# Attention over gathered tokens on one core: one transpose for the reciprocal sums of two pairs of heads, and the norms of the first of two pairs moved later

## The chip, the cores and the metric

The kernel runs on one core of a Trainium2 chip. The metric is the device time of one execution in microseconds; lower is better. An engine is named as the profile names it: PE is TensorE, DVE is VectorE, ACT is ScalarE, POOL is GpSimd, and SP is the engine whose queue issues most of the transfers. PEld is the weight load of TensorE, which overlaps its products.

## The reference, cut to what matters

There are B = 16 sequences (called batches here) of T = 1024 tokens with D = 512 features. A mask of zeros and ones marks about half of the tokens of each. The same projection serves as query, key and value, for 8 heads of 64 features:

```python
q = xt @ Wq.T                                     # (B, T, D)
qh = q.reshape(B, T, NH, dk).transpose(0, 2, 1, 3)
scores = scale * jnp.einsum('bhqd,bhkd->bhqk', qh, qh)
logits = (scores * cmask + (1.0 - cmask) * NEG) * rmask
attn = jax.nn.softmax(logits, axis=-1)
ctx = jnp.einsum('bhqk,bhkd->bhqd', attn, qh)
out = ctx @ Wo.T                                  # (B, T, D), added to x
```

A masked key gets no weight. A masked query has all logits zero, so its row is the plain mean over all tokens. Only the unmasked tokens need the attention proper.

## The kernel before, in words

**Tiles.** For each batch the unmasked tokens (at most C = 544) are gathered to the front: four full tiles of 128 rows and a tail of 32. Heads are worked on in pairs: 8 heads are 4 pairs, numbered p = 0 to 3, and a group g of four heads is two pairs (0 and 1, or 2 and 3). The scores of one head and one tile of 128 rows are a block of 128 x 544, made on PE by products in fp16 of a high and a low part (`scores`, L611), then exponentiated on ACT with a sum along the row (L615). The tails of four heads are packed into one such block (L586, L590) and split by DVE into two parts (L595, L596), which four transfers `pt` spread (L602, L603). `attend` multiplies the probabilities by the values: L629 for the full tiles, L632 for the tails. ACT then copies the context of the pair, still without the division by the row sums, to a tile `c` of 128 x 544 (L636): its partitions are the 2 x 64 features of the pair, its columns the tokens.

**The division.** The sums lie along the partitions (one token to a partition), but the context needs them along the columns. Three steps do this for each pair:

- `recip_sums` (L644) puts the corrected sums of the pair into ten columns of a tile `rcol` (128 x 128) and takes the reciprocals, on DVE: two heads, five blocks of tokens each.
- `recip_rows` (L661) transposes the whole `rcol` by a product with the identity (L665), copies the ten rows that matter to `rr` (L668), writes them to DRAM (`rd`, L670) and reads them back with two transfers (`rb`, L673), each of which broadcasts one head's 544 values over 64 partitions. `rb` has two buffers.
- `norm` (L677) multiplies `c` by `rb` (L696), puts the means of padded queries in (L697), and splits the result into a high and a low half in fp16: `ch` and `cl` for the full tiles (L699, L700), a column block of `ct` for the tail (L701, L702). For pairs 0 to 2 the multiplication also waits for the last score or query product issued before it (`self.beat`).

`project` multiplies `ch` and `cl` by the output weights (L712, 12 products a tile of 128 rows, three for each pair), DVE adds the old x (L717), and POOL scatters the rows. `project_tail` does the same for the tails of a group of up to three batches.

**The order of the work.** `run` goes through the batches in one software pipeline. A batch has 18 slots, four for each pair and two for the packed tails (slots 2 and 13). In each slot the scores of two heads are issued; between them come the products of the block before (`attend`), and a share of the list `m`. That list holds the rest: query blocks (L443) and their transposes to values (L489) of the next batch, the gathered x of the next batch transposed (L420) and split (L380 on ACT, L381 on DVE), and the projection of the batch before. Steps in `free` are tied to a slot and come before its scores. For pairs 0 and 1 and 2 the sums come two slots after the pair's last, the rows three, and the norm of pairs 0 and 1 seven. The norm of pair 2 (`second`) and sums, rows and norm of pair 3 (`sums`, `rows`, `third`) are done in the next batch:

```python
m = sums + pk(b, 1) + x[:2] + second + x[2:4] + rows + x[4:]
```

and later `third` stands between two parts of query block 1: `q(1, 0) + v(0) + third + q(1, 1)`. A query block ends with a mask that DVE applies to columns 384 to 543 (L449); the transpose of the fourth column block waits for it. The last batch has its own list, and `last` ends the kernel.

The calls give a rough order only. A scheduler then places the instructions on each engine, moving ready ones ahead of waiting ones; what is marked with `high_priority` (the copy `rr`, the splits of x, the addition L717) goes first. Once placed, each engine works in that fixed order and waits at the head of its queue. All transfers named above are in the one queue of SP.

Of the kernel before, what the change touches and what calls it, by code (L numbers as in the profile page):

```python
# [10 lines left out]
F32 = mybir.dt.float32  # L11
# [8 lines left out]
P = 128  # L20
# [3 lines left out]
DK = 64  # L24
NP = H // 2
DC = D // P
# [4 lines left out]
C = 544  # L31
# [18 lines left out]
class Fast:  # L50
# [593 lines left out]
    def recip_sums(self, b, p):  # L644

        nc, s = self.nc, self.st[b]
        hs, g = slice(2 * p, 2 * p + 2), p // 2
        corr = s["corr"][g]
        r = self.rcol[p % 2][:, :10]
        m = r.rearrange("p (h k) -> p h k", k=5)  # L650
        nc.vector.tensor_tensor(m[:, :, :4], s["z"][:, hs, :],
                                corr[:, p % 2 * 2:p % 2 * 2 + 2].unsqueeze(2).broadcast_to([P, 2, 4]), ALU.subtract)
        for h in range(2):
            q = (2 * p + h) % HG
            rows = slice(q * CT, (q + 1) * CT)
            nc.vector.tensor_tensor(m[:CT, h, 4:5], s["zt"][rows, g:g + 1], corr[rows, HG:], ALU.subtract)
        nc.vector.tensor_scalar(r, r, 1e-35, 1.0 / SX, ALU.max, ALU.mult)
        nc.vector.reciprocal(r, r)
        nc.vector.tensor_tensor(m, m, self.hit[:, b, :].unsqueeze(1).broadcast_to([P, 2, 5]), ALU.mult)

    def recip_rows(self, b, p):  # L661

        nc, s = self.nc, self.st[b]
        pt = self.pm([P, P])
        nc.tensor.transpose(pt, self.rcol[p % 2], self.ident)  # L665
        rr = self.sb([10, P], F32, "rr", 2)
        with self.tc.high_priority(offset=HPO):
            nc.vector.tensor_copy(rr, pt[:10])  # L668
        rd = self.dram.tile([10, P], F32, tag="rd", name="rd")
        nc.sync.dma_start(out=rd, in_=rr)  # L670
        rb = self.sb([P, C], F32, "rb", 2)
        for k in range(2):
            nc.sync.dma_start(out=rb[k * DK:(k + 1) * DK, :], in_=rd[5 * k:5 * k + 5, :].rearrange("k t -> (k t)")[:C]  # L673
                              .unsqueeze(0).broadcast_to([DK, C]))
        s.setdefault("rb", {})[p] = rb

    def norm(self, b, p):  # L677
        nc, s = self.nc, self.st[b]
# [127 lines left out]
    def last(self, b, todo):  # L806

        for f in self.soon + todo:
            f()
        self.soon = []  # L810
        while self.urgent or self.spare:
            self.issue()
        self.paced = False
        s = self.st[b]
        self.recip_sums(b, 3)
        pos = []
        for i in range(2):
            t = self.ps_s.tile([P, 2, D], F32, tag="s", name="pss")
            pos += [t[:, k, :] for k in range(2)]
        pos.append(self.pm([P, D]))  # L820
        for i in range(4):
            self.product(s["ch"], s["cl"], slice(i * P, (i + 1) * P), pos[i], range(3))
            if i == 0:
                self.recip_rows(b, 3)
        self.norm(b, 3)
        for i in range(4):
            self.project(b, i, pos[i], range(3, DC))
        self.project_tail(b, pos[4])

    def run(self, flag):  # L830
        B = self.B
        L = lambda f, *a: lambda: f(*a)
# [3 lines left out]
        N = len(S)  # L836
# [93 lines left out]
        if True:  # L930
            for b in range(B + 1):
                o, n = b - 1, b + 1
# [2 lines left out]
                    break  # L935
                free, sums, rows, third, tail, rest = {}, [], [], [], [], []
                if b:
                    sums, rows, third = [(0, L(self.recip_sums, o, 3))], [(0.1, L(self.recip_rows, o, 3))], [(0, L(self.norm, o, 3))]
                if n < B:
                    if b in tails:  # L940
                        free[0] = [L(self.late, o, 4)]
# [1 line left out]
                    for x in rests.get(b, []):  # L943
                        free.setdefault(0, []).extend(L(self.late, x, j) for j in range(5, 9))
                        rest += [(0, L(self.rest, x, j)) for j in range(5, 9)]
                second = [(0, L(self.norm, o, 2))] if b else []
                P_ = (lambda *i: project(o, *i)) if b else (lambda *i: [])
                pk, tp, bt = ((lambda o, g, f=f, c=c: [(c, L(f, o, g))]) for f, c in ((self.peaks, 0), (self.top, 0.1), (self.bottom, 0.1)))
                new = [g for g in groups if b == g[0] - 2], [g for g in groups if b == g[0] - 1]
                if n < B:  # L950
                    q, x, v = (lambda e, g: query(n, e, g)), xt(n)[2 if b == 0 else 0:], (lambda e: value(n, e))
                    tc, tv = ((lambda g, f=f, c=c: [(c, L(f, n, g))]) for f, c in ((self.tail_copy, 0), (self.value_tail, 0.25)))
                    rng = [(0, L(self.range_x, n, c)) for c in range(DC)]
                    ahead = b + 2 < B
                    hot, index = ([(c, L(f, b + 2))] if ahead else [] for f, c in ((self.hot, 0), (self.index, 0.2)))
                    take = [(0, L(self.gather, b + 2, j)) for j in range(5)] if ahead else []
                    m = sums + pk(b, 1) + x[:2] + second + x[2:4] + rows + x[4:]
                    for g in new[0]:
                        m += [(0, L(self.active, *g))]
                    m += q(0, 0) + tp(b, 1) + q(0, 1)  # L960
                    for g in new[0]:
                        m += [(0.3, L(self.slots, *g))]
                    for g in new[1]:
                        m += [(0, L(self.facts_sums, *g))]
                    m += bt(b, 1) + q(1, 0) + v(0) + third + q(1, 1)
                    for g in new[1]:
                        m += [(0.1, L(self.facts_end, *g))]
                    m += tc(0) + rng[:2] + tail + v(1) + P_(0) + tv(0) + rest + P_(1) + hot + rng[2:] + q(2, 0) + index
                    m += pk(n, 0) + q(2, 1) + tp(n, 0) + P_(2) + take + v(2) + q(3, 0) + bt(n, 0)
                    m += q(3, 1) + tc(1) + [(0, L(self.means, n))] + P_(3) + v(3) + tv(1)  # L970
                    if b == 0:
                        k = next(k for k, (c, f) in enumerate(m) if f is index[0][1])
                        for c in range(DC):
                            m.insert(k + 1 + 3 * c, (0, L(self.split, "o", c)))
                else:

                    places = [("xi", 8), ("xa", 13)]
                    come = [[L(self.late, x, j, *places[k % 2]) for j in range(5, 9)] for k, x in enumerate(rests[b])]
                    leave = [[L(self.rest, x, j) for j in range(5, 9)] for x in rests[b]]
                    free[0] = [L(self.late, b, 4)] + come[0]  # L980
                    for c, l in zip(come[1:] + [[]], leave):
                        free[0] += c + l
                    m = second + sums + pk(b, 1) + [(2.6, L(self.project_means, b))] + rows + [(0.6, lambda: None)]
                    m += tp(b, 1) + [(0.6, lambda: None)] + bt(b, 1) + [(1.2, lambda: None)] + third + [(1.2, lambda: None)] + P_(0, 1, 2, 3)
                if b == 1:
                    m += [(0, L(self.range_w, "o", c)) for c in range(DC)]
# [2 lines left out]
                if b == 0:  # L989
                    m = begin + m  # L990
# [22 lines left out]
                for st, (p, i) in enumerate(S):  # L1013
                    soon, self.soon = self.soon, []
                    for f in soon + free.get(st, []):
                        f()
                    if i is None:
                        self.scores(b, p, None)
                    else:
                        ps = [self.scores(b, 2 * p, i)]  # L1020
                        if i == 2 and whole:
                            whole.pop()()
                    fill(share[st][0], st == N - 1)
                    if i is not None:
                        ps.append(self.scores(b, 2 * p + 1, i))

                    for _ in range(1 if b < B - 2 else -(-len(self.urgent + self.spare) // (N - st))):
                        self.issue()

                    if i in (0, 2):  # L1030
                        ready, todo = todo, []
                    elif i in (1, 3):
                        for f in ready[1::-1] + ready[2:]:
                            f()
                        ready = []
                    fill(share[st][1])
                    if i is not None:
                        todo.append(L(self.attend, b, p, i, ps))
                    if i == 3:
                        (whole if p < 3 else todo).append(L(self.attend, b, p, 4, None))  # L1040
                        if p < 3:
                            free.setdefault(st + 2, []).append(L(self.recip_sums, b, p))
                            free.setdefault(st + 3, []).append(L(self.recip_rows, b, p))
                            if p < 2 or b == B - 1:
                                free.setdefault(min(st + 7, N - 1), []).append(L(self.norm, b, p))
                self.st.pop(b - 4, None)
        bad = self.const.tile([1, 1], F32, name="bad")
        self.nc.vector.tensor_reduce(bad, self.ok[0:1, :], AX.X, ALU.add)
# [145 lines left out]
```

## Time and profile before

| what | value |
|---|---|
| median of 3 runs | 1074.26 us (1073.34 to 1080.06) |
| the profiled execution | 1082.2 us |
| its span | 1080.5 us, mean granted clock of PE 0.993 |
| PE, DVE, ACT, POOL busy | 1053.5, 739.3, 679.0, 317.5 us |
| transposes of the sums (L665) | 64, 20.8 us |
| copies `rr` (L668) | 64, 17.7 us |
| multiplications by `rb` (L696) | 64, 45.9 us |
| transfers `rd`, `rb`, `pt`, `xx` | 64, 128, 128, 256 |

The page gives busy time by engine, the share of each in the chain that ended last, and the groups of instructions with the idle time of the engine just before them. In the timeline a row has its start and length in microseconds from the start of the span, the engine, the line, the operation, output and inputs, and the count where equal ones are merged; a bracket gives the idle time of the engine before it and what ended this. The length of a PE row is longer than its slot in the queue, since products overlap: what one costs is read from start to start.

### The profile page before, as it was taken

How to read it: one execution, taken by the hardware profiler on the slowest of the kernel's cores; microseconds unless marked ns; L12 is line 12 of the kernel's file. 1: busy time of each engine (PE TensorE's matmuls, PEld its weight loads, DVE VectorE, ACT ScalarE, POOL GpSimd, SP SyncE). 2: the span in 40 equal slices, each digit the busy share in tenths (PEclk: the TensorE clock that was granted, in tenths of full speed). 3: DMA queues.
4: the chain of work that ended last, by engine and by line, in shares of the span. 5: the costliest groups of instructions: out<-in, count | busy, mean ns of one | idle time of the engine just before them, and what ended most of it. 6: DMA issues, size and time to landing. Idle time of an engine off the chain costs nothing.

```text
span 1080.5 us, 23254 instructions
## 1 busy us (share of the span) xinstructions
PE 1053.5 (98%) x8386; PEld 698.3 (65%) x8386; DVE 739.3 (68%) x2375; ACT 679.0 (63%) x1722; POOL 317.5 (29%) x303
## 2 busy tenths in 40 slices
PE   7899999999999999999999999999999999999996
PEld 6566666666666666666666666666666676666553
DVE  5698668676765767767685676958577676757553
ACT  4786667566666756657666666766667565655550
POOL 2101022232401222332322323223232322234643
PEclk8999999999999999999999999999999999999999
DMA  5756565546655654666556566554765555466652
GB/s 186 218 152 167 138 175 157 170 139 191 173 141 156 170 168 145 189 192 172 175 143 194 168 182 188 154 172 134 211 190 171 179 149 154 134 179 195 193 165 85
DMA packets 78122, 181.35 MB, mean 168 GB/s; under 512 B 15008, under 2 KB 16800, under 8 KB 78000
## 3 DMA queue, kind: packets, MB, share of 16 engines
q1 hardware_dynamic: 56816, 111.62, 37.1%
q0 software_dynamic: 21184, 68.18, 19.8%
q8 instruction: 68, 1.11, 0.4%
q14 instruction: 54, 0.44, 0.1%
HBM read 92.34 MB, written 33.91 MB: 117 GB/s over the span
## 4 chain that ended last, share of the span: by engine, by line
PE 88%; DVE 5%; ACT 3%; issue 2%; DMA 1%; POOL 0%; another core or an unknown queue 0%; POOLq 0%; SPq 0%; ACTq 0%; DVEq 0%
PE pav L629 23%; PE pss L611 21%; PE pm L443 15%; PE pm L712 14%; PE pm L420 3%; PE pav L632 3%; PE pm L489 2%; PE pss L586 2%; PE pm L665 1%; ACT p L615 1%; PE pm L511 1%; ACT xm L365 1%; PE warm L303 1%; ACT p L590 1%; DVE p L596 1%
## 5 line engine op out<-in xcount | busy, mean ns | idle before, releaser
L615 ACT ACTIVATE p<-pss,nm 128x544 f32<-128x544 f32 x512 | 365.9, 717 | 231.8 <-PE pss L611 221.8
L611 PE MATMUL pss<-xx 128*128 128x272 f16 x2048 | 314.1, 280 | 3.2 <-ACT p L615 2.3
L629 PE MATMUL pav<-p,v 128*64 128x272 f32 x2048 | 273.5, 401 | 0.0
L611 PEld LDWEIGHTS <-xx 128*128 128x128 f16 x2048 | 193.1, 100 | 77.8 <-issue 31.3
L629 PEld LDWEIGHTS pav<-p,v 128*64 128x64 f32 x2048 | 131.9, 136 | 94.4 <-issue 34.0
L796 POOL DMA_INDIRECT y_out<-xa,idx x68 | 68.7, 1011 | 283.2 <-PE pss L611 83.9
L443 PE MATMUL pm<-xh,wqh 128*128 128x274 f16 (+1 forms) x512 | 143.7, 281 | 3.1 <-DVE xa L717 2.2
L443 PE MATMUL pm<-xh,wql 128*128 128x274 f16 (+1 forms) x512 | 143.2, 280 | 0.0
L443 PE MATMUL pm<-xl,wqh 128*128 128x274 f16 (+1 forms) x512 | 143.1, 280 | 0.0
L335 POOL DMA_INDIRECT xa<-x_in,idx x68 | 76.4, 1124 | 174.6 <-PE pss L611 64.4
L443 PEld LDWEIGHTS <-wqh 128*128 128x128 f16 x1024 | 99.1, 99 | 26.0 <-issue 7.1
L796 POOL DMA_INDIRECT y_out<-xi,idx x60 | 76.8, 1280 | 121.9 <-PE pss L611 43.3
L615 ACT ACTIVATION_READ_ACCUMULATOR p<-pss,nm 128x1 f32 x512 | 103.5, 202 | 0.0
L717 DVE SCALAR_TENSOR_TENSOR xa<-pm,xa 128x512 f32<-128x512 f32 x60 | 41.4, 690 | 87.7 <-PE pm L712 83.6
L335 POOL DMA_INDIRECT xi<-x_in,idx x60 | 62.1, 1036 | 109.8 <-PE pss L611 39.0
L712 PE MATMUL pm<-woh,ch 128*128 128x512 f16 x240 | 91.1, 379 | 0.0
L712 PE MATMUL pm<-woh,cl 128*128 128x512 f16 x240 | 91.0, 379 | 0.0
L712 PE MATMUL pm<-wol,ch 128*128 128x512 f16 x240 | 91.0, 379 | 0.0
L446 ACT ACTIVATE q<-pm 128x272 f32<-128x272 f32 (+1 forms) x128 | 50.6, 395 | 60.0 <-PE pm L443 52.5
L712 PEld LDWEIGHTS <-ch 128*128 128x128 f16 x480 | 46.4, 98 | 45.7 <-issue 1.3
L365 ACT ACTIVATE xm<-xm 128x1024 f32<-128x1024 f32 (+1 forms) x62 | 62.5, 1009 | 1.9 <-DMA xm<-x_nat_in 1.9
L783 DVE TENSOR_TENSOR xi<-xi,ub 128x512 f32<-128x512 f32 (+1 forms) x60 | 41.3, 691 | 30.5 <-PE pss L611 28.5
(191 smaller groups left out, 1562.5 us busy)
## 6 DMA issues: line engine op xcount, KB each, us to landing
xx<-hl SPq DMA_DIRECT2D x256, 136.0 KB
xm<-x_nat_in SPq DMA_DIRECT2D x56, 512.0 KB
rb<-rd SPq DMA_DIRECT2D x128, 136.0 KB
pt<-c SPq DMA_DIRECT2D x64, 136.0 KB
pt<-p SPq DMA_DIRECT2D x64, 136.0 KB
ub<-ud SPq DMA_DIRECT2D x16, 256.0 KB
xi<-x_nat_in SPq DMA_DIRECT2D x8, 256.0 KB
xa<-x_in,idx POOLq DMA_INDIRECT x68
```

Of the source, the lines that this page charges most:

```text
L335: dma = self.nc.gpsimd.indirect_dma_start(out=tile[:n], out_offset=None, in_=self.x, in_offset=bass.IndirectOffsetOnAxis(ap=idx, axis=0))
L365: self.nc.scalar.activation(s["xm"][k], s["xm"][k], AF.Copy, accum_out=s["ms2"][:, k:k + 1])
L420: self.pe = nc.tensor.transpose(pt[:, c, :], x[:n, c * P:(c + 1) * P], self.ident[:n, :n]).ins
L443: self.beat = nc.tensor.matmul(pq, lhsT=w[:, c, e * P:(e + 1) * P], rhs=xx[:, c, cols], start=(k == 0), stop=(k == 3 * DC - 1)).ins
L446: nc.scalar.activation(s["q"][:, e, cols], pq, AF.Copy, scale=1.0 / (SX * SW))
L611: self.beat = nc.tensor.matmul(pt[:, g, :CH], lhsT=xx[:, 2 * k, i * P:(i + 1) * P], rhs=xx[:, 2 * k + a, g * CH:(g + 1) * CH], start=(a == ...
L615: self.exp = [nc.scalar.activation(t.rearrange("p (g c) -> p g c", g=2), pt[:, :, :CH], AF.Exp, bias=s["nm"][p // HG][:, p % HG:p % HG + 1 ...
L629: nc.tensor.matmul(s["pav"][k * DK:(k + 1) * DK, g, :CH], lhsT=s["v"][p][:, i, k * DK:(k + 1) * DK], rhs=ps[k][:, cols], start=(i == 1), s ...
L712: nc.tensor.matmul(po[:cols.stop - cols.start], lhsT=a[:, e, cols], rhs=w[:, e, :], start=(e == 0 and k == 0), stop=(e == DC - 1 and k == 2))
L717: self.nc.vector.scalar_tensor_tensor(x, po, 1.0 / (SX * SW), x, ALU.mult, ALU.add)
L783: self.once(self.nc.vector.tensor_tensor(x[:n], x[:n], s["ub"][:n], ALU.add), self.beat)
L796: dma = self.nc.gpsimd.indirect_dma_start(out=self.out, out_offset=bass.IndirectOffsetOnAxis(ap=idx, axis=0), in_=x, in_offset=None)
```

## The change

`rcol` holds the sums of two pairs, twenty columns, and one transpose turns them into rows, for the pairs 0 and 1 together and for 2 and 3 together. The rows of pair 0 wait for those of pair 1, and the rows of pair 2 for those of pair 3 in the next batch. The four transfers `rb` are issued in a row. So the norms move too:

- pair 0: from slot 11 to slot 14, one slot before that of pair 1, which stays at slot 15;
- pair 2: from the start of the next batch to stand beside pair 3 (`third`);
- in the last batch, pair 2: from its last slot to `last`, where the projection is now begun with the pairs 0 and 1 alone and completed with 2 and 3.

```diff
-        r = self.rcol[p % 2][:, :10]
+        r = self.rcol[p // 2][:, 10 * (p % 2):10 * (p % 2) + 10]
...
-        nc.tensor.transpose(pt, self.rcol[p % 2], self.ident)
-        rr = self.sb([10, P], F32, "rr", 2)
+        nc.tensor.transpose(pt, self.rcol[p // 2], self.ident)
+        rr = self.sb([20, P], F32, "rr", 2)
         with self.tc.high_priority(offset=HPO):
-            nc.vector.tensor_copy(rr, pt[:10])
-        rd = self.dram.tile([10, P], F32, tag="rd", name="rd")
+            nc.vector.tensor_copy(rr, pt[:20])
+        rd = self.dram.tile([20, P], F32, tag="rd", name="rd")
         nc.sync.dma_start(out=rd, in_=rr)
-        rb = self.sb([P, C], F32, "rb", 2)
-        for k in range(2):
-            nc.sync.dma_start(out=rb[k * DK:(k + 1) * DK, :], in_=rd[5 * k:5 * k + 5, :].rearrange("k t -> (k t)")[:C]
-                              .unsqueeze(0).broadcast_to([DK, C]))
-        s.setdefault("rb", {})[p] = rb
+        for o in (p - 1, p):
+            rb = self.sb([P, C], F32, "rb", 2)
+            for k in range(2 * (o % 2), 2 * (o % 2) + 2):
+                nc.sync.dma_start(out=rb[k % 2 * DK:k % 2 * DK + DK, :], in_=rd[5 * k:5 * k + 5, :].rearrange("k t -> (k t)")[:C]
+                                  .unsqueeze(0).broadcast_to([DK, C]))
+            s.setdefault("rb", {})[o] = rb
...
         for i in range(4):
-            self.product(s["ch"], s["cl"], slice(i * P, (i + 1) * P), pos[i], range(3))
+            self.product(s["ch"], s["cl"], slice(i * P, (i + 1) * P), pos[i], range(2))
             if i == 0:
                 self.recip_rows(b, 3)
-        self.norm(b, 3)
+        for k in (2, 3):
+            self.norm(b, k)
         for i in range(4):
-            self.project(b, i, pos[i], range(3, DC))
+            self.project(b, i, pos[i], range(2, DC))
...
-                    sums, rows, third = [(0, L(self.recip_sums, o, 3))], [(0.1, L(self.recip_rows, o, 3))], [(0, L(self.norm, o, 3))]
+                    sums, rows, third = [(0, L(self.recip_sums, o, 3))], [(0.1, L(self.recip_rows, o, 3))], [(0, L(self.norm, o, k)) for k in (2, 3)]
...
-                second = [(0, L(self.norm, o, 2))] if b else []
...
-                    m = sums + pk(b, 1) + x[:2] + second + x[2:4] + rows + x[4:]
+                    m = sums + pk(b, 1) + x[:2] + x[2:4] + rows + x[4:]
...
-                    m = second + sums + pk(b, 1) + [(2.6, L(self.project_means, b))] + rows + [(0.6, lambda: None)]
+                    m = sums + pk(b, 1) + [(2.6, L(self.project_means, b))] + rows + [(0.6, lambda: None)]
...
                         if p < 3:
                             free.setdefault(st + 2, []).append(L(self.recip_sums, b, p))
+                        if p == 1:
                             free.setdefault(st + 3, []).append(L(self.recip_rows, b, p))
-                            if p < 2 or b == B - 1:
-                                free.setdefault(min(st + 7, N - 1), []).append(L(self.norm, b, p))
+                            for k in range(2):
+                                free.setdefault(st + 6 + k, []).append(L(self.norm, b, k))
```

## The prediction

> **What bounds the kernel now.** I read first the page's busy shares and the granted clock, then the chain that ended last, then who TensorE waited for, and then the timeline of the places that the change touches.
>
> ```profile
> PE 1053.5 (98%) x8386; PEld 698.3 (65%) x8386; DVE 739.3 (68%) x2375; ACT 679.0 (63%) x1722; POOL 317.5 (29%) x303
> ...
> PE 88%; DVE 5%; ACT 3%; issue 2%; DMA 1%; POOL 0%; another core or an unknown queue 0%; POOLq 0%; SPq 0%; ACTq 0%; DVEq 0%
> ```
>
> TensorE is busy for 98% of the span and carries 88% of the chain; its clock was granted in full (0.993). So an instruction taken from TensorE is worth its own slot in the queue, and a wait put in front of one costs its full length. VectorE (DVE, 68%) has room on average, but works in order. The list of waits shows how little TensorE waits for it now:
>
> ```profile
> PE pm L443 <- DVE xa L717: 2.2, 5, 1.1
> PE pm L489 <- DVE q L449: 1.5, 4, 0.4
> ```
>
> (who waited for whom: us in all, times, longest.) All of TensorE's waits together are some 18 us, over a third of them before the first batch. The loss to look for is therefore a new wait of TensorE for VectorE.
>
> **The change part by part.**
>
> *Transposes.* The group of L665 has 64 of them, four a batch; 32 go: that of pair 0 and that of pair 2 (the sums of a group of four heads now share one). What one costs the queue is read from start to start:
>
> ```profile
> 343.15 0.28 PE L443 MATMUL pm<-xh,wql 128*128 128x274 f16 x1
> 343.44 0.33 PE L665 MATMUL pm<-ident,rcol 128*128 128x128 f32 x1
> 343.60 1.09 PE L611 MATMUL pss<-xx 128*128 128x272 f16 x8
> ```
>
> From L443 to L611 it is 0.45 us; without a transpose between them it is 0.12 (309.53 to 309.65). So this one costs 0.33. Done in the same way for every removed one against its nearest like: pair 0's cost 0.16 each (16 of them, 2.6 us), pair 2's 0.34 in eight batches, 0.21 in five and 0.10 in three (4.1 us). Upper end 6.7 us. The lower end counts only the slot after the transpose, 0.165 x 32 = 5.3, since in front of pair 2's some of the gap may be a wait that the next product inherits. I take **-6.0 us**.
>
> *Row copies and transfers.* With each transpose go a copy rr (277 ns on DVE) and a transfer rd of 5 KB, and the queue of SP waits 32 times less for an rd; the transfers rb stay 128, but are issued four in a row, each 0.55 us on SP. A rule of the Trainium skill (SBUF — State Buffer, "The DMA setup-cost knee") speaks loudly for this part: a transfer costs some 2 us whatever its size, so 32 small ones less would be 64 us. The row of the readers decides against it:
>
> ```profile
> L696 DVE TENSOR_TENSOR c<-c,rb 128x544 f32<-128x544 f32 x64 | 45.9, 718 | 9.6 <-SPq L1164 5.0 <-issue 2.6 <-PE pss L611 2.0
> ```
>
> Of 64 multiplications by rb only two lost time to a transfer, both in the last batch's work (5.0 at the very end, 2.6 for the pair before). The 2 us are hidden everywhere else, by the products of the following pair, and I count 0, not -64.
>
> *Norm of pair 2 moved to stand beside that of pair 3.* This is where the loss is. It was done early in the next batch, among the splits of x (L381), where DVE waits for ACT anyway; now both norms stand ahead of the mask L449 of query block 1. Batch 4, DVE, then PE:
>
> ```profile
> 304.90 0.72 DVE L696 TENSOR_TENSOR c<-c,rb 128x544 f32<-128x544 f32 x1
> ...
> 307.22 0.18 DVE L702 TENSOR_TENSOR ctl<-c,cth 128x32 f16<-128x32 f32 x1
> ...
> 308.55 0.16 DVE L659 TENSOR_TENSOR rcol<-rcol,hit 128x10 f32<-128x10 f32 x1
> 310.28 0.33 DVE L449 TENSOR_TENSOR q<-q,hr 128x160 f32<-128x160 f32 x1 [1.57 <-ACT q L446]
> ```
>
> ```profile
> 309.65 0.63 PE L611 MATMUL pss<-xx 128*128 128x272 f16 x4
> 310.11 0.88 PE L489 MATMUL pm<-ident,q 128*128 128x128 f32 x4
> 310.83 0.63 PE L611 MATMUL pss<-xx 128*128 128x272 f16 x4
> ```
>
> The last of the four transposes of L489 reads columns that L449 masks, and the four took 0.72 us here against 0.43 at 304.80, so PE already meets L449 with no slack. Behind that transpose stand the scores of the next pair and the whole projection. In the order in which the changed kernel issues, all twelve instructions of the two norms stand before L449. One norm in a dense stretch costs 0.64 (L696), 0.31, 0.34, 0.11, 0.61, 0.21 from start to start: 2.2 us. What DVE has idle between L696 and L449 takes up part: 0.97 us in batch 1, 1.24 in 3, 1.67 in 4, 1.25 in 7 and 1.64 in 9, 12 and 13. So L449 slips by 1.25, 0.95, 0.55, 0.95 and three times 0.55: **+5.4 us**, all on PE. In batches 2, 5, 8, 11 and 14 a tail's projection stands between, and L489 comes 4 to 5.5 us after L449: nothing. In 6 and 10 the index work of new batches (L228 to L239) changes places with the second norm, and the wait of 0.44 stays. Bounds: 0, if the norms find room earlier; 7 x 2.2 = 15, if the idle time can't be used. The row stands near the idle reading, so 5.4. The new wait of norm 2 for a product (the beat) falls on a product that ended at about 305.8, when norm 3's first instruction is just done: 0 to 0.2 a batch, inside this.
>
> *Norm of pair 0 moved from slot 11 to 14, beside that of pair 1.* Queued behind it are now the split of the tail's probabilities (L595, L596) and their transfers pt on SP, for which L632 waits. In batch 4 L595 starts at 339.86 after 1.40 us idle; two instructions of norm 0 (1.0 us) fit into this, then the order puts L480 ahead of L596, which slips by 0.4. The last pt, issued at 342.72, would go at 343.1; with 3.2 us to landing (from the end of the kernel, below) it is there at 346.3, and L632 comes at 347.00. Hidden, with 0.7 to spare; beyond that each 0.1 costs 1.5 over the batches. I take **+0.5** (0 to 5). In front of slot 14 DVE gets the same 2.2 us back, where nobody waits for it: no gain.
>
> *Last batch, first part.* There rb of pair 3 landed only at 1022.4, and the projection of the batch before started at 1022.86. Norm 3 now follows norm 2, so its halves come about 2.2 us later than the products of 1024.8 want them: 1.9 of stall, of which some 0.9 is idle already (PE waits 0.87 for ACT at 1026.9). **+1.2** (0 to 2).
>
> *The end.* Before, 27 of 36 products covered rows and norm of pair 3; now 18 cover rows and two norms.
>
> ```profile
> 1061.01 0.32 SPq L670 DMA_DIRECT2D rd<-rr  x1
> 1062.23 1.09 SPq L673 DMA_DIRECT2D rb<-rd  x2
> ```
>
> ```profile
> 1066.00 0.72 DVE L696 TENSOR_TENSOR c<-c,rb 128x544 f32<-128x544 f32 x1 [5.02 <-SPq L1164]
> ...
> 1068.25 0.18 DVE L702 TENSOR_TENSOR ctl<-c,cth 128x32 f16<-128x32 f32 x1
> ...
> 1071.86 0.38 PE L712 MATMUL pm<-woh,ctl 128*64 128x512 f16 x1
> ```
>
> The transpose now comes after six products, not nine, so 0.65 earlier: rb of pair 2 issued at 1061.58 and 1062.13. From the second issue to the norm it was 3.2 us (1062.78 to 1066.00): norm 2 runs from 1065.35 to 1067.8, norm 3 after it, its first half ready 1.6 later, at 1069.4. PE has used up its 30 products without pairs 2 and 3 at about 1065.0, waits for the nine of pair 2 and again for pair 3, and then has 21 x 0.216 = 4.5 left: 1073.9 against 1072.2, **+1.7**. By the rule named above an rb of 139 KB would take 2 + 0.32 = 2.3 us, the end +0.8; I keep the row.
>
> Sum: -6.0 + 5.4 + 0.5 + 1.2 + 1.7 = **+2.8 us**. The profiled execution took 1082.2 (span 1080.5); it would be 1085.0. It lies 8 above the median of 1074.3; the differences carry over: 1077.1.
>
> **The rivals.** *Not slower.* If DVE reaches L449 on time, the stall of 5.4 is gone: -2.6, about **1071.5**. For it: DVE is idle 32%, and loses norm 2 at the start of the batch. Against: the stretch from 301.3 to 308.7 is dense, and L449's place in the queue is fixed. It decides where the second norm adds less than 1.7 us, which is what three or four of the seven batches have free; up to there L449 moves by nothing.
>
> *Transfers late.* The rb of pair 3 are now the third and fourth in a row, 1.1 us later. In batch 4 the second was issued at 299.25; +1.1 and 3.2 to landing give 303.6, and the norm wants it at 304.90. If the transfers take 2 us longer among the traffic of mid-kernel, norm 3 heads the queue and blocks DVE, and each of some nine batches loses 1 to 1.5 more: **1089**. Against: no row of L696 waits for rb in mid-kernel.
>
> That the change does less than it says is ruled out: the transposes are written out, 32 of 64.
>
> **How the numbers follow.** Forecast (0 to +9 us) 0.52; not slower (-8 to 0) 0.28; late transfers or a wait that I overlooked (+9 to +18) 0.17; better than all of this 0.03. The range goes from 1068 (gain of 6.7 with no stalls) to 1087 (stall of 10 and late pt). A measurement of this kernel can tell about 1%, 10.7 us: faster 0.03, same 0.80, slower 0.17.
>
> **What would show it.** L665 32 times. L489's wait for DVE L449 from 1.5 us in 4 to about 7 in 9 to 11. L696 with two new waits at the end. Wrong: a wait of L632 for DMA, of L696 for rb in mid-kernel, or no growth at L489.

## The result, and the profile after

The changed kernel takes 1081.58 us (median of 12 runs, 1077.62 to 1085.08) against 1077.44 for the kernel before (12 runs, 1073.34 to 1080.06): a ratio of 1.0040, with a 95% interval of 1.0026 to 1.0054, or +4.1 us. The forecast was +2.8 us. The sign and the range held. Of the terms of the sum, those of the transposes, the mask and the end came out near what was said; that of the tail's transfers did not, and one cost stood in no term: a slower clock behind a wait.

The page of the changed kernel, busy shares:

```profile
PE 1047.6 (97%) x8354; PEld 692.4 (64%) x8354; DVE 725.7 (67%) x2343; ACT 680.9 (63%) x1722; POOL 312.0 (29%) x303
```

TensorE runs 32 instructions fewer and is busy for 5.9 us less, yet the kernel is longer: what was taken off came back as waits. The chain that ended last breaks off at once in this profile and carries nothing; the list of TensorE's waits has to do its work. (Who waited for whom: us in all, times, longest.)

```profile
PE pm L489 <- DVE q L449: 4.5, 7, 1.3
PE pav L632 <- DMA pt<-p: 3.2, 3, 1.2
PE pm L489 <- DVE sc L251: 2.1, 3, 0.8
PE pm L713 <- DVE ch L700: 1.6, 2, 1.4
PE pss L713 <- DVE xh L700: 1.5, 1, 1.5
```

Three things are new. L489 waits 4.5 + 2.1 = 6.6 us in ten places where it waited 1.5 in four (in batches 1, 3 and 7 the wait ends with L251, which reads a small product just ahead of L449 and stands behind the norms like it; before, it was itself waiting for TensorE there). L632 waits for the tail's transfers, which it never did. And the products of the last batch wait for the norms. By groups:

```profile
L697 DVE TENSOR_TENSOR c<-c,rb 128x544 f32<-128x544 f32 x64 | 46.2, 722 | 16.8 <-PE pss L586 6.0 <-DMA rb<-rd 5.8 <-SPq L1166 4.9
L489 PE MATMUL pm<-ident,q 128*128 128x128 f32 x256 | 42.6, 279 | 7.4 <-DVE q L449 4.5 <-DVE sc L251 2.1 <-ACT q L446 0.4
L665 PE MATMUL pm<-ident,rcol 128*128 128x128 f32 x32 | 10.4, 326 | 0.0
```

L665 is there 32 times. The norm's first line (L696 before, L697 now) waits 5.8 us for its rows, in three places: 1.0 and 1.4 in mid-kernel (at 399.5 and 562.0) and 3.3 in the last batch. So two of the three signs of being wrong that the prediction had named are here: L632 waits for a transfer, and the norm for its rows in mid-kernel.

Batch 4, the norms ahead of the mask, on VectorE:

```profile
301.85 0.73 DVE L697 TENSOR_TENSOR c<-c,rb 128x544 f32<-128x544 f32 x1
302.63 0.72 DVE L697 TENSOR_TENSOR c<-c,rb 128x544 f32<-128x544 f32 x1
...
306.72 0.19 DVE L703 TENSOR_TENSOR ctl<-c,cth 128x32 f16<-128x32 f32 x1
...
307.28 0.17 DVE L659 TENSOR_TENSOR rcol<-rcol,hit 128x10 f32<-128x10 f32 x1
307.37 0.32 DVE L449 TENSOR_TENSOR q<-q,hr 128x160 f32<-128x160 f32 x1
```

and on TensorE:

```profile
306.21 0.63 PE L611 MATMUL pss<-xx 128*128 128x272 f16 x4
306.67 0.52 PE L489 MATMUL pm<-ident,q 128*128 128x128 f32 x3
307.74 0.33 PE L489 MATMUL pm<-ident,q 128*128 128x128 f32 x1 [0.55 <-DVE q L449]
307.91 0.63 PE L611 MATMUL pss<-xx 128*128 128x272 f16 x4
```

Before, L449 came 1.57 us after the work ahead of it, held only by ScalarE. Now it follows that work directly, and the fourth transpose waits 0.55: the number that the prediction had worked out for this batch.

In the last batch the products of the projection wait 1.44 us for norm 3's first half, with waits of 0.21 and 0.20 just before, and then the clock falls. A table by stretches shows it (start to end and length; then busy us and instructions of PE, PEld, DVE, ACT and POOL; then the granted clock of TensorE, the share of the DMA engines and GB/s):

```profile
1019.64:1023.05 3.41, 1.57 (x6) 0.32 (x5) 3.34 (x9) 0.25 (x2) 2.32 (x3) 1.00 0.99 367
1023.05:1026.46 3.41, 3.41 (x13) 1.49 (x13) 1.30 (x3) 1.19 (x3) 0.14 (x1) 0.50 0.35 103
```

Half the clock for 3.41 us is 1.7 us lost. A little earlier the profile of the kernel before has a wait that this one doesn't have; the second profile of the changed kernel (after2, below) has it at the same product. The kernel before, then after2:

```profile
1017.27 0.62 PE L611 MATMUL pss<-xx 128*128 128x272 f16 x4 [1.69 <-ACT p L615]
```

```profile
1020.70 0.62 PE L611 MATMUL pss<-xx 128*128 128x272 f16 x4 [1.69 <-issue]
```

This wait comes in five of the 14 profiles. It belongs to the execution and not to the change.

The end of the kernel, queue of SP, then VectorE, then TensorE:

```profile
1059.13 0.32 SPq L670 DMA_DIRECT2D rd<-rr  x1
1060.50 2.39 SPq L674 DMA_DIRECT2D rb<-rd  x4
```

```profile
1063.96 0.72 DVE L697 TENSOR_TENSOR c<-c,rb 128x544 f32<-128x544 f32 x1 [4.86 <-SPq L1166]
```

```profile
1065.62 0.39 PE L713 MATMUL pss<-woh,xh 128*128 128x512 f16 x1 [1.55 <-DVE xh L700]
...
1072.52 0.38 PE L713 MATMUL pss<-woh,xl 128*128 128x512 f16 x1
```

From the tail's first product to the last instruction of TensorE it is 1057.20 to 1072.90, 15.7 us; before it was 1058.44 to 1072.24, 13.8. The end costs 1.9 us.

### The profile page after: what moved, and what is told of

Its sections match the earlier page's. It is cut to its first block, busy times and chain, and to the rows that moved or that the text cites. A ratio compares the mean times of both kernels' runs of the same rounds, so it can differ in the third digit from the quotient of the medians.

```text
span 1081.4 us, 23056 instructions
## 1 busy us (share of the span) xinstructions
PE 1047.6 (97%) x8354; PEld 692.4 (64%) x8354; DVE 725.7 (67%) x2343; ACT 680.9 (63%) x1722; POOL 312.0 (29%) x303
## 5 line engine op out<-in xcount | busy, mean ns | idle before, releaser
L611 PEld LDWEIGHTS <-xx 128*128 128x128 f16 x2048 | 190.3, 99 | 82.2 <-issue 38.6
L335 POOL DMA_INDIRECT xa<-x_in,idx x68 | 74.0, 1088 | 169.1 <-PE pss L611 114.5
L797 POOL DMA_INDIRECT y_out<-xi,idx x60 | 74.4, 1240 | 120.6 <-PE pss L611 43.4
L713 PE MATMUL pm<-woh,ch 128*128 128x512 f16 x240 | 91.1, 380 | 1.6 <-DVE ch L700 1.6
L713 PE MATMUL pm<-woh,cl 128*128 128x512 f16 x240 | 91.2, 380 | 0.2 <-DVE cl L701 0.2
L713 PE MATMUL pm<-wol,ch 128*128 128x512 f16 x240 | 91.2, 380 | 0.0
L713 PEld LDWEIGHTS <-ch 128*128 128x128 f16 x480 | 46.3, 98 | 47.6 <-DVE ch L700 2.4
L381 DVE SCALAR_TENSOR_TENSOR xl<-pm,xh 128x512 f16<-128x512 f32 (+1 forms) x75 | 43.1, 607 | 41.9 <-ACT xh L380 41.8
```

What stands on the lines that cost most here:

```text
L335: dma = self.nc.gpsimd.indirect_dma_start(out=tile[:n], out_offset=None, in_=self.x, in_offset=bass.IndirectOffsetOnAxis(ap=idx, axis=0))
L381: self.xs = nc.vector.scalar_tensor_tensor(self.xl[dst], src, SX, self.xh[dst], ALU.mult, ALU.subtract).ins
L611: self.beat = nc.tensor.matmul(pt[:, g, :CH], lhsT=xx[:, 2 * k, i * P:(i + 1) * P], rhs=xx[:, 2 * k + a, g * CH:(g + 1) * CH], start=(a == ...
L713: nc.tensor.matmul(po[:cols.stop - cols.start], lhsT=a[:, e, cols], rhs=w[:, e, :], start=(e == 0 and k == 0), stop=(e == DC - 1 and k == 2))
L797: dma = self.nc.gpsimd.indirect_dma_start(out=self.out, out_offset=bass.IndirectOffsetOnAxis(ap=idx, axis=0), in_=x, in_offset=None)
```

## Experiments

All kernels but the repeats of the changed one are written from one source in which a switch says which pairs share a transpose. In it lines of the page stand one higher (L490 for L489, L633 for L632), from the rows product on ten to twelve higher (L675 for L665, L708 for L697, L724 for L713), and in no_rb0 two or three more. The kernel before was run beside them and took 1077.1, 1076.3 and 1083.3 us in the three sets, each on another chip; so between sets only ratios are compared. "Mid" below is the time from the second group of L586 in batch 0 (at about 80 us) to that of batch 14 (about 980), less the same in the profile of the kernel before: it leaves the start out, whose length varies (see the last section). It is one profile each, and between two profiles of the changed kernel it differed by 2.5 us.

**First set: which half pays.**

```diff
+M01, M23, MLAST = True, False, False
...
+    def merged(self, b, p):
+        return M01 if p < 2 else (M23 if b < self.B - 1 else MLAST)
...
+        ps = (p - 1, p) if self.merged(b, p) else (p,)
-        nc.tensor.transpose(pt, self.rcol[p // 2], self.ident)
+        nc.tensor.transpose(pt, self.rsum(b, p), self.ident)
```

> Only the pairs 0 and 1 share a transpose; pairs 2 and 3 as before. Theory (the loss is VectorE's order: a late mask in front of the transposes to values, a late split in front of the tail's transfers, two norms at the end): 16 transposes less, -2.6 us, against about +3 us of waits of the tail's products (L632 in the kernel before) for the transfers pt: between -1 and +2 us against before; the transposes to values (L489) wait for the mask as little as before, 1.5 us in all. Rival (the loss is in the one queue of SP, four transfers rb in a row): about half of the whole change, +2 us, with the row multiplications (L696) waiting for rb.

Measured: 1.0041 (1.0027 to 1.0056), +4.4 us. A miss for both. The waits of TensorE show why:

```profile
PE pm L675 <- DVE rcol L661: 3.5, 10, 0.5
...
PE pav L633 <- DMA pt<-p: 0.8, 1, 0.8
```

In ten batches the transpose of pair 2 meets its own sums a third of a microsecond late. Those sums (the work of L651 to L659 in the kernel before) now stand behind norm 0 in VectorE's queue, since norm 0 has moved into the slot where they are made. In the whole change nobody sees this, because there pair 2 has no transpose of its own. So half of the change is not half of its effect: the half that should have gained had a reader that the other half removes.

The other half alone:

```diff
+M01, M23, MLAST = False, True, True
```

> Only the pairs 2 and 3 share a transpose, in the last batch too; pairs 0 and 1 as before. Theory: -2.7 to -4.1 us for 16 transposes, +5.3 for the late mask in batches 1, 3, 4, 7, 9, 10, 12 and 13, +1.9 at the end, +1 in the first part of the last batch: +4 to +5.5 us against before; the transposes to values wait 6 to 7 us for VectorE; no wait of the tail's products for pt. Rival (SP's queue): about half of the whole change, +2 us, and the waits for the mask are made good elsewhere.

Measured: 1.0047 (1.0031 to 1.0063), +5.1 us, as expected.

```profile
PE pm L490 <- DVE q L450: 4.4, 8, 1.0
...
PE pm L490 <- DVE sc L252: 2.1, 3, 0.8
```

The waits at the mask are those of the whole change (6.5 against 6.6 us), and L633 has no wait for pt at all.

The third kernel of the set lets the mask go first:

```diff
-                    m += bt(b, 1) + q(1, 0) + v(0) + third + q(1, 1)
+                    m += bt(b, 1) + q(1, 0) + v(0) + q(1, 1) + third
```

> The changed kernel, with both norms asked for after the second half of query block 1 and not before it, so that the mask comes ahead of the second norm in VectorE's order. Theory: the wait of the transposes to values falls from 6.6 to about 1.5 us, and the time by 5 us against the changed kernel: about -1 us against before. Rival (SP's queue): the wait goes, but the time stays at +3 to +4 us, since the transfers are the same.

Measured: 1.0068 (1.0045 to 1.0091), +7.3 us; both theories missed.

```profile
PE pav L633 <- DMA pt<-p: 4.5, 5, 1.7
...
PE pm L490 <- DVE q L450: 2.9, 4, 1.8
...
PE pm L724 <- DVE cth L713: 2.6, 5, 0.8
```

L490's wait falls from 6.6 to 2.9, of which 1.8 is one place in batch 10. But in the five batches in which the projection of a tail stands right behind, that projection now waits for the norms (L724 for cth, 2.6 us), and the waits for pt have grown. The stall had not been removed; it had been given to the next reader.

The price of a transpose by itself:

```diff
+M01, M23, MLAST = False, False, False
...
         nc.tensor.transpose(pt, self.rsum(b, p), self.ident)
+        nc.tensor.transpose(pt, self.rsum(b, p), self.ident)
```

> The kernel before with every one of the 64 transposes of the sums issued twice to the same place; nothing else. What a transpose is worth by itself: if the slot after it is its cost, 64 x 0.165 = +10.6 us; if the gap in front of it belongs to it as well, up to +13. If transposes are hidden in gaps that TensorE has anyway, less than +4 us.

Measured: 1.0073 (1.0052 to 1.0095), +7.9 us for 64 more, 0.12 each (0.09 to 0.16). That lies between the cases named. Mid gives 6.21 us for the 56 in it, 0.111 each, and grows evenly, by some 0.22 in each half batch.

This is the price of a second transpose right behind the first. What is saved when one is left out is another number, and the profiles hold it. Here are three starts of the packed tails in batches 4 and 5, in the kernel before and in the changed one:

```profile
338.29 0.65 PE L586 MATMUL pss<-xx 128*32 128x272 f16 x16
363.17 0.65 PE L586 MATMUL pss<-xx 128*32 128x272 f16 x16
401.61 0.65 PE L586 MATMUL pss<-xx 128*32 128x272 f16 x16
```

```profile
335.22 0.65 PE L586 MATMUL pss<-xx 128*32 128x272 f16 x16
359.77 0.65 PE L586 MATMUL pss<-xx 128*32 128x272 f16 x16
398.06 0.65 PE L586 MATMUL pss<-xx 128*32 128x272 f16 x16
```

In the first stretch none of the six profiles of this table has a wait of TensorE, in the second each has the same one of 0.20 us (h01_late and move2 are described below):

| kernel | first stretch, transposes of pairs 2 and 3 | second stretch, pairs 0 and 1 |
|---|---|---|
| before | 24.88 us | 38.44 us |
| move2: none shared, norm 2 moved | 24.88 | 38.44 |
| h01_late: pair 0's gone | 24.88 | 38.30 |
| h23: pair 2's gone | 24.55 | 38.44 |
| changed: both gone | 24.55 | 38.29 |
| double_t: each twice | 25.09 | 38.66 |

So a transpose of pair 2 that is left out saves 0.33 us here, and one of pair 0 0.15, while a doubled one adds 0.11. The transpose of pair 2 starts 0.06 us after the sums that it reads are done (343.38 to 343.44 in the kernel before): part of its 0.33 may be a wait for them, and this goes with it. A doubled one comes behind that wait.

**Second set: the moves one by one.** h01 again with both norms a slot later, so that neither pair 2's sums nor the tail's split has them ahead:

```diff
-                            for k, d in enumerate((6, 7)):
+                            for k, d in enumerate((7, 8)):
                                 free.setdefault(st + d, []).append(L(self.norm, b, k))
```

> Pairs 0 and 1 share a transpose, as in h01, but norm 0 stands in slot 15 and norm 1 in slot 16, one slot later, so that the sums of pair 2 and the tail's split in slot 14 have nothing new ahead of them. Theory (h01's loss was norm 0 in slot 14: TensorE's transpose of pair 2 met rcol 0.33 us late in ten batches, 3.5 us, and pt came late at times): the wait of the rows product for rcol is gone, and with 16 transposes at 0.11 each less the kernel takes 1.5 to 2 us less than the kernel before. Rival (the four transfers of rows issued one after the other, or the larger rd, cost it): +3 to +4.5 as h01.

Measured: 0.9992 (0.9981 to 1.0004), -0.9 us; 5.3 less than h01, with the same transfers. The waits for rcol and pt are gone, and what is left at the mask is what the kernel before had (1.4 against 1.5):

```profile
PE pm L490 <- DVE q L450: 1.4, 4, 0.4
```

That is the theory's case, a little short of the 1.5 to 2 that it named; the interval reaches from -2.0 to +0.4. The rival, that four row transfers in a row cost by themselves, falls for this kernel.

The same step in the whole change:

> The changed kernel with norm 0 in slot 15 and norm 1 in slot 16. Theory (norm 0 ahead of the split of the tail makes pt late): no wait of L633 for pt but for a stray one, and +1 to +2 against the kernel before, some 2.5 us less than the changed kernel. Rival (pt is late because of the row transfers that share the queues): the waits for pt stay, +4.

Measured: 1.0054 (1.0035 to 1.0072), +5.8 us. A miss, nearer to the rival: norm 0 out of the way of the split did not help. One wait for pt stayed, in batch 3, and it was longer than in the changed kernel:

```profile
281.94 0.79 PE L633 MATMUL pav<-pt,vt 128*128 128x272 f32 x4 [2.41 <-DMA pt<-p]
```

The table by stretches, columns as above, tells what it led to:

```profile
279.08:282.50 3.42, 1.01 (x8) 0.69 (x6) 3.42 (x14) 1.01 (x4) 0.20 (x1) 1.00 0.90 230
282.50:285.91 3.41, 3.41 (x12) 1.54 (x11) 0.68 (x2) 1.42 (x3) 0.94 (x1) 0.50 0.69 145
```

After 2.41 us of waiting the granted clock is 0.50 for 3.41 us. Between the marks at 275 and 300 us this kernel loses 4.0 us against the profile of before: 2.4 of wait, and 1.6 more, which is about what half a clock takes from 3.41 us (1.7). The waits of 0.85 and 1.51 in two profiles of the changed kernel at the same place left the clock at 1.00.

Norm 2's place alone, every pair with its own transpose:

```diff
-                second = [(0, L(self.norm, o, 2))] if b else []
+                second = []
...
-                    sums, rows, third = [(0, L(self.recip_sums, o, 3))], [(0.1, L(self.recip_rows, o, 3))], [(0, L(self.norm, o, 3))]
+                    sums, rows, third = [(0, L(self.recip_sums, o, 3))], [(0.1, L(self.recip_rows, o, 3))], [(0, L(self.norm, o, k)) for k in (2, 3)]
```

> The kernel before, every pair with a transpose of its own, but norm 2 stands beside norm 3, ahead of the mask of query block 1. Theory (the mask is what the change pays for): L490 waits for L450 as in the changed kernel, 6 to 7 us in all, and the kernel takes 5 to 6 us more than before; with h23's +5.0 that leaves at most 1 to 2 us for the 15 transposes. Rival (norm 2's place costs nothing and the rows of two pairs in one transfer do): 0 to +1.

Measured: 1.0080 (1.0058 to 1.0102), +8.6 us, more than expected.

```profile
PE pm L675 <- DVE rcol L661: 3.4, 1, 3.4
PE pm L490 <- DVE q L450: 3.2, 8, 0.5
...
PE pm L490 <- DVE sc L252: 2.0, 3, 0.7
```

The mask shows: L490 waits 5.2 us, 3.7 more than before. The surplus is a single wait of 3.4 us in the last batch (at 1028.5): a rows product that the change shares away waits for its sums, and these stand behind norm 3, which waits for its rows:

```profile
1025.31 0.73 DVE L708 TENSOR_TENSOR c<-c,rb 128x544 f32<-128x544 f32 x1 [4.21 <-DMA rb<-rd]
```

Again a reader that exists only in the half change. Behind this wait the granted clock was 0.50 from 1029.22 to 1032.63, 1.7 us more. Mid, which leaves both out, is +4.4.

The last batch as before, the rest as in the change:

```diff
+M01, M23, MLAST = True, True, False
```

> The changed kernel, but in the last batch pairs 2 and 3 keep a transpose each and norm 2 its early place. Theory (the end costs 1.9 of the changed kernel's 4.2): +2 to +2.5 against the kernel before, and the last products run 13.8 us after the first as before. Rival (the end is paid for elsewhere, or is hidden): +4.

Measured: 1.0044 (1.0028 to 1.0059), +4.7 us, beside no run of the changed kernel; its runs went from 1075.6 to 1090.9, and its profile had a wait of 3.5 us for pt in batch 3. Inconclusive, so it was run again in the next set.

**Third set, beside the changed kernel itself.**

> The changed kernel once more, beside the three that follow, so that they are compared with it on the same chip: +4 against the kernel before. In the stretch of batch 3 around 280 us both theories expect L632 to wait for pt again (0.85 in its first profile).

Measured: 1.0021 (1.0009 to 1.0033), +2.3 us, less than in the first comparison (its interval began at 1.0026). The wait for pt in batch 3 came again, 1.51 us; those of batches 7 and 10 did not.

> As no_end: the changed kernel, with the last batch's pairs 2 and 3 as before. Theory (the end costs what its two profiles differ by): 1.5 to 2 us less than the changed kernel of this call. Rival (the end is hidden): the same as the changed kernel.

Measured: 1.0009 (0.9997 to 1.0022), 1.3 us less than the changed kernel of the same set. That is near the theory's 1.5 to 2, but the two intervals overlap; what shows the end is the trace (15.7 and 15.8 us in the two profiles of the changed kernel, 13.8 in those of no_end and no_end2).

The rows of pair 0 not transferred, everything else in place:

```diff
-            rb = self.sb([P, C], F32, "rb", 2)
-            for k in range(2):
+            rb = self.flat if o == 0 else self.sb([P, C], F32, "rb", 2)
+            for k in range(0 if o == 0 else 2):
```

> The changed kernel, but the rows of pair 0 are not transferred (its norm multiplies by a constant 0.001 in place of them): two transfers of 136 KB less in each batch, everything else in its place, norm 0 in slot 14 as well. Theory (pt comes late where four row transfers meet the gathers and the xm load, with the DMA engines busy 90% and more; norm 0's place alone does little): no wait of L633 for pt, and 2 to 3 us less than the changed kernel. Rival (norm 0 ahead of the split delays pt): the waits for pt stay, the same time as the changed kernel.

Measured: 1.0007 (0.9998 to 1.0016), 1.5 us less than the changed kernel (here too the two intervals overlap), and no wait for pt. The last transfers of the tail in batch 3, queue of SP, with the product that reads them: the kernel before,

```profile
279.25 0.60 SPq L603 DMA_DIRECT2D pt<-p  x1
```

```profile
283.56 0.75 PE L632 MATMUL pav<-pt,vt 128*128 128x272 f32 x4
```

the changed kernel of this set,

```profile
281.83 1.17 SPq L603 DMA_DIRECT2D pt<-p  x2
```

```profile
288.44 0.76 PE L632 MATMUL pav<-pt,vt 128*128 128x272 f32 x4 [1.51 <-DMA pt<-p]
```

and without the rows of pair 0:

```profile
282.67 1.16 SPq L606 DMA_DIRECT2D pt<-p  x2
```

```profile
287.51 0.75 PE L635 MATMUL pav<-pt,vt 128*128 128x272 f32 x4
```

In the first and third the last transfer (begun at 279.25, and half of 1.16 after 282.67) is in time for a product 4.3 us later that doesn't wait. In the changed kernel it takes 6.0 (from 282.42 to 288.44). Norm 0 is at the same place in the last two; so it is not a later issue but a longer way, and two row transfers less shorten it. What is not settled is why h01 and h01_late, with the same four transfers in a row, have no such wait in batch 3: their small rd landed earlier there (2.64 and 2.53 us from its issue to that of the first rb, against 2.90 to 3.65 in the seven profiles of kernels that share all and transfer all), and I have no run that tells this from the traffic of the other pairs.

The last kernel puts together what the runs point to: norms 0 and 1 a slot later, the last batch as before, and norms 2 and 3 behind the mask, except where a tail's projection would wait for them:

```diff
+M01, M23, MLAST = True, True, False
...
-                    m += bt(b, 1) + q(1, 0) + v(0) + third + q(1, 1)
+                    m += bt(b, 1) + q(1, 0) + v(0) + (third + q(1, 1) if b in tails else q(1, 1) + third)
...
-                            for k, d in enumerate((6, 7)):
+                            for k, d in enumerate((7, 8)):
```

> The changed kernel with norm 0 and norm 1 one slot later, the last batch as before, and norms 2 and 3 behind query block 1's second half (the mask) except in batches where a tail's projection follows. Theory (what the change loses is the mask's wait, 5 us, the end, 1.9, and pt): L490's waits are back to 2 us, what is left of the loss is pt in batch 3, and the kernel takes -2 to +2 against the kernel before. Rival (the wait moves on to another engine, as it did in mask_first): +3 or more.

Measured: 0.9959 (0.9944 to 0.9974), -4.4 us, better than both kernels and than the theory's range.

```profile
PE pm L490 <- DVE q L450: 1.7, 4, 0.5
...
PE pav L633 <- DMA pt<-p: 0.3, 1, 0.3
```

Both waits are nearly back at what the kernel before had. What is left to gain from is the 31 transposes that it removes; how much each brings here was not measured by itself. The 4.4 us come from five executions, and mid is only -2.1 in its one profile.

## Why the prediction was right, and where it was not

- **Transposes, -6.0: right.** The profiles without one save 0.15 us for pair 0's and 0.33 for pair 2's where TensorE waits for nothing new (the table at double_t); the prediction had read 0.16 and, in eight batches, 0.34. Over the whole of mid, h23 and move2 place norm 2 alike and differ in the shared transposes: with the listed waits taken off, pair 2's come to 0.25 a piece. That makes 16 x 0.15 + 16 x 0.25 = 6.4 us, an estimate from single profiles. The 0.111 of double_t is no measure for it.
- **Transfers, 0 instead of the rule's -64 (the Trainium skill, SBUF — State Buffer, "The DMA setup-cost knee"): right about the rule, not about the zero.** 32 small transfers less brought nothing like 2 us each (h01_late, with 16 fewer, is at -0.9 us in all). But the row transfers do cost where the DMA engines are about 90% busy: the pt wait of batch 3.
- **Norm of pair 2 ahead of the mask, +5.4: right.** L489 waits 6.6 instead of 1.5 us, +5.1: 4.6 in the seven batches that the prediction named (1, 3, 4, 7, 9, 12, 13), 0.9 in batch 10, where 0.44 was to stay and became 1.32, and 0.4 less elsewhere. In the second profile batch 10 stays at 0.41 and all of it is +4.3. h23 has the same waits and move2 most of them; best2 takes them away and wins.
- **Norm of pair 0 in slot 14, +0.5 "hidden, with 0.7 to spare": wrong in the reason.** The last pt was issued 4.1 us after L586 of its slot in batch 3, before 4.40: norm 0 did not hold it back. It landed later, 3.2 us of waits in the first profile and 1.5 in the second. Norm 0 out of slot 14 (after_late) leaves it; two transfers less (no_rb0) remove it. The step carried the landing time over from the quiet end of the kernel into its busiest stretch. Missed altogether was that pair 2's sums stand behind norm 0; in the change nobody waits for them, in h01 it costs 3.5 us.
- **Last batch, first part, +1.2: the wait right, the clock left out.** The products wait 1.44 + 0.21 + 0.20 = 1.85 us for norms (1.9 was worked out), and the wait of 0.87 for ScalarE is gone as was said. What the sum didn't have is the 1.7 us of the slow clock behind it. From the scores at 1017.14 to those at 1028.18 it takes 3.0 us longer than before. In the second profile the norms come in time, the clock stays full, and the same stretch is 0.2 shorter than before.
- **The end, +1.7: right,** +1.9 by the trace. Norm 2 came at 1063.96 instead of 1065.35, but the tail's first product was 1.24 earlier as well.

With what was measured, and the transposes left at -6.0, the sum is -6.0 + 5.1 + 3.2 + 3.0 + 1.9 = +7.2 for the first profile. Two waits of the profile before, 1.69 and 1.14 us, which the first profile lacks and the second has too (1.69 and 1.00), take 2.8 off: +4.4, where its trace is 6.0 longer than that of before from the second group of L586 on. For the second it is -6.0 + 4.3 + 1.5 - 0.2 + 1.9 = +1.5, and its trace is 2.6 longer. So 1 to 1.6 us are in no term, and the cause of these stays open. Measured were +4.1 and +2.3. The mechanism of the largest loss, the mask, was right. That +2.8 came so near is in part luck: the pt waits that were taken for hidden (1 to 2.7 us more than the 0.5), the slow clock (1.7) and what is in no term were left out, and how much of them an execution has differs from one to the next.

Of the rivals, "not slower" falls: the second norm does not fit into VectorE's idle time ahead of the mask. "Transfers late" comes true in a smaller form. Norm 3 did not block VectorE in nine batches; rows came late in three places (5.8 us of VectorE, one of them 3.3 in the last batch), and the loss went by way of pt, not of the norm.

## What to carry to other kernels

Before an operation is put together with a later one, list everyone who stands behind it in its engine's queue at the new place, and the readers of that: here most of the loss was 5 us at one mask, and another order in nine batches took it away. When a change is tested in halves, look for readers that exist only in the half; h01 and move2 both lost 3.4 us or more to a transpose that the full change does not have. And do not take what leaving out an instruction saves from a run that doubles it: the doubled transpose cost 0.11 us, the one left out saved 0.15 or, where it had stood close behind what it reads, 0.33. Compare the same stretch with and without it, where the waits are alike.

## What the runs showed of the hardware

**TensorE's clock fell by half for a step of 3.41 us after a step in which it had been idle for about half.** In each of the 14 profiles all changes of the granted clock lie on one grid of 3.41 us, and it is either 1.00 or 0.50. Up to TensorE's last product there are 4332 steps at full clock. In 18 of them TensorE was busy, by the profile's count, for less than 1.5 us, and a slow step followed each time; of 15 with 1.5 to 1.95 us three were followed by one (1.57 us in the changed kernel's last batch); of the others none. So the length of a wait alone does not decide: 1.44 us with two small ones beside it was enough there, while 1.51 us across the border of two steps in batch 3 of the second profile left the clock at 1.00. The 2.41 us of after_late cost 4.0 in all. The Trainium skill (TensorE: Matmul & The Clock Gate, "The HAM clock gate") has the array at half rate after at least one idle window of about 3.4 us. The length agrees with the step here; idle throughout it did not have to be. By the page's rule the 2.41 us would have cost themselves alone, and the measurement decides.

**The start makes much of the spread between executions.** The two profiles of the changed kernel are 7.4 us apart by the second group of L586 in batch 0 (76.36 and 83.72). The stretches of the first, columns as above:

```profile
16.00:24.00 8.00, 7.52 (x75) 6.16 (x73) 6.47 (x20) 4.28 (x11) 1.00 (x1) 1.00 0.63 195
40.00:48.00 8.00, 7.40 (x67) 4.66 (x65) 6.12 (x19) 6.93 (x20) 0.00 (x0) 1.00 0.51 141
```

and of the second:

```profile
16.00:24.00 8.00, 7.92 (x61) 7.10 (x61) 4.30 (x12) 3.74 (x9) 0.00 (x0) 0.66 0.23 68
40.00:48.00 8.00, 4.72 (x31) 2.35 (x29) 1.07 (x2) 2.75 (x9) 0.00 (x0) 0.62 0.72 182
```

In the second, TensorE waits for the first rows of x (1.85 us) and close behind for something that the profile doesn't show on this core (1.95 us), and again for xx (3.28 us), and the clock in these stretches is 0.66 and 0.62. The profile of the kernel before had both in part (0.64 and 0.79), the first one of the changed kernel had neither; so two spans of almost equal length (1080.5 and 1081.4) hid a loss of 6.0 us after the first 80. Marks after the start compare what the spans could not.
